# Turning, scaling and storing an expert's results later, and in three groups, in a mixture-of-experts kernel

## The chip, the cores and the metric

The kernel runs on one core of one Trainium2 chip. The metric is the device time of one execution in microseconds (us). The core's engines are called as in the profile: PE is TensorE (matmul), PEld its weight load, DVE is VectorE, ACT is ScalarE, POOL is GpSimd, and SP is the engine that issues most of the DMA transfers. SPq, ACTq and so on are the sequencers of these engines.

## The reference

There are 2048 tokens (8 batches of 256) of width 1024. Each batch is multiplied by one of eight adapter matrices; the result goes through a feed-forward block with one shared expert and 16 routed experts, two for each token, and is added to x.

```python
y = einsum('bsi,boi->bso', x, weight[itok])          # (8, 256, 1024), one adapter for each batch
gu_s = y2 @ shared_w_gate_up.T                       # y2: (2048, 1024)
shared = (silu(g_s) * u_s) @ shared_w_down.T         # inner width 1024
probs = softmax(y2 @ gate_w.T)                       # 16 experts
topk_vals, topk_idx = top_k(probs, 2)                # combine: the two values, normed to sum 1
gu = einsum('th,eih->eti', y2, w_gate_up)            # inner width 256
out_e = einsum('eti,ehi->eth', silu(g) * u, w_down)
return x + einsum('eth,te->th', out_e, combine) + shared
```

All of it is fp32. The kernel does not compute every expert for every token: it gathers the tokens of each expert, and computes those alone.

## The kernel before

Every fp32 operand of a matmul is made into two parts, `hi` and `lo`: `split` casts the source to `hi` on ACT (L88) and subtracts on DVE (L89) to get `lo`. A product is three matmuls, hi x hi, hi x lo and lo x hi (`mm3`, L139 to L141).

The work comes in stages: the adapter products, and the shared expert for the first half of the tokens, with the routing between (up to about 444 us of the profiled span); then the routed experts, to about 745 us; then the shared expert for the second half of the tokens, and the sum of all parts.

The experts are taken in the order of their load, so that each place n in this order has a fixed number of columns, `CAPS[n]`: 304 for n = 0 down to 264 for n = 10, and 256 for the last five. In each turn of the main loop over n (L1216):

- `expert_rows(n + 2)` gathers the tokens' rows on POOL (L839).
- `expert_up(n + 1)` loads four gate/up weights (`wgu`), each through `load_w`, and makes the gate and up products of expert n + 1.
- `expert_out(n)` loads two down weights (`wd`) through `load_w` and makes the down products of expert n. Where `CAPS[n]` is over 256 this is `expert_down_columns`.
- `expert_yt(n + 2)` turns the gathered rows (L226, into the tile `tt`) and splits them (L88, L89, tile `yte`).

`load_w` (L118) issues a weight's DMA on SP, in the order of the loads (tile `st`, four buffers), and splits it into the tile `hl` (five and two buffers). Then it takes the next entry of the list `between` and runs it, so that its instructions stand behind the subtraction of that load on DVE:

```python
        end = split(hl[:, 0, :], hl[:, 1, :], st)
        work = between.pop(0) if between else None
        if work:
            with tc.issue_after(end):
                work()
```

`issue_after(x)` makes the instructions of the block that run on the engine of x stand behind x. Otherwise the order on each engine is made by a planner with a timeline of its own (`schedule_with_timeline_sim`), which takes the earlier instruction of the program among those that it holds ready. Loads can run several ahead of the products that use them.

`expert_down_columns` has the results of expert n with the tokens along the free axis. Eight products (128 result columns each, 48 matmuls in all) go through the banks `acc` (seven of them); ACT copies each into `ot` (L920). Then DVE turns the 32 x 32 blocks from `ot` to `o` in two instructions (L922), ACT multiplies each 32 tokens by the routing weight in place (L928, nine or ten instructions), and SP stores `o` to the DRAM table `os_d` in four DMAs (L936), one for each quarter of the partitions. `ot` lies in the first and `o` in the second of the two `raw` tiles: there is one of each for all experts. The trace names both `raw`.

The turnings stand right behind the copies. The scalings come by `between`: its six entries meet the six loads that follow `expert_out(n)`, the four gate/up weights of expert n + 2 and the two down weights of expert n + 1. The last three of them carry three, three, and the remaining scalings; the stores stand behind the last.

For n = 13 and 14, `between` is filled with other work (`block`, L1209), which writes into the `raw` tiles again.

Of the kernel before, what the change touches and what calls it, by code (L numbers as in the profile page):

```python
# [17 lines left out]
P = 128  # L18
# [17 lines left out]
ROW0 = [sum(ROWS[:n]) for n in range(E + 1)]  # L36
# [5 lines left out]
def adapter_moe_kernel(ctx: ExitStack, tc: tile.TileContext, xT, x, itok, wc, gate, wgu, wd, sgu, sd, out):  # L42
    nc = tc.nc
# [27 lines left out]
    os_d = dram.tile([ZROW + 16, H], F32, tag="os_d", name="os_d")  # L71
# [7 lines left out]
    def bank():  # L79
        turn[0] += 1  # L80
        return banks[turn[0] % 7]
# [19 lines left out]
    between = []  # L101
# [36 lines left out]
    def mm3(ps, lhs, rhs, first, last):  # L138
        nc.tensor.matmul(ps, lhs[0], rhs[0], start=first, stop=False)  # L139
        nc.tensor.matmul(ps, lhs[0], rhs[1], start=False, stop=False)  # L140
        last_product[0] = nc.tensor.matmul(ps, lhs[1], rhs[0], start=False, stop=last).ins  # L141
# [705 lines left out]
    def expert_id(n):  # L847
        return nc.values_load(order[0:1, n : n + 1], engines=(mybir.EngineType.SP,), min_val=0, max_val=E - 1)
# [20 lines left out]
    def load_wd(e):  # L869
        return [load_w(wd[ds(e, 1), fi].rearrange("a p f -> p (a f)")) for fi in range(2)]  # L870
# [12 lines left out]
    def expert_down(po, at, w, off, c=1.0):  # L883
        o = po.tile([P, 1024], F32, tag="o", bufs=3, name="o")
        for h in range(2):
            ps = bank()
            for fi in range(2):
                mm3(
                    ps,
                    [at[:, l, fi, off : off + P] for l in range(2)],  # L890
                    [w[fi][:, l, h * 512 : (h + 1) * 512] for l in range(2)],
                    fi == 0,
                    fi == 1,
                )
            nc.scalar.activation(
                o[:, :].rearrange("p (a b j) -> p b a j", a=4, b=8)[:, 4 * h : 4 * h + 4],
                ps[:, :].rearrange("p (b a j) -> p b a j", b=4, a=4),
                AF.Copy,
                scale=c,
            )  # L900
        return o
# [3 lines left out]
    def expert_down_columns(n, at, w):  # L905
        m, rows, nt = CAPS[n], ROWS[n], ROWS[n] // 32
        ot, o = (r[:, :, :].rearrange("p c n -> p (c n)") for r in raw)
        ot = ot[:, : 8 * rows].rearrange("p (b t i) -> p b t i", b=8, i=32)
        o = o[:, : nt * 256].rearrange("p (t f) -> p t f", t=nt)
        for b in range(8):  # L910
            ps = bank()
            for fi in range(2):
                mm3(
                    ps[:, :m],
                    [w[fi][:, l, b * P : (b + 1) * P] for l in range(2)],
                    [at[:, l, fi, :] for l in range(2)],
                    fi == 0,
                    fi == 1,
                )
            nc.scalar.copy(ot[:, b], ps[:, :rows].rearrange("p (t i) -> p t i", i=32))  # L920
        for k in range(2):
            nc.vector.transpose(o[:, :, k * P : (k + 1) * P].rearrange("p t (b j) -> p b t j", b=4), ot[:, 4 * k : 4 * k + 4])  # L922

        def scaled(ts, end):
            def work():
                with tc.issue_after(last_cast[0]):
                    for t in range(nt)[ts]:
                        nc.scalar.activation(o[:, t], o[:, t], AF.Copy, scale=cwt[:, t, n : n + 1])  # L928
                if end:
                    store()  # L930

            return work

        def store():
            for a in range(4):
                nc.sync.dma_start(  # L936
                    os_d[ROW0[n] : ROW0[n] + rows, 256 * a : 256 * a + 256].rearrange("(t i) f -> i t f", i=32),
                    o[32 * a : 32 * a + 32],
                )

        between[:] = [None, None, None, scaled(slice(0, 3), False), scaled(slice(3, 6), False), scaled(slice(6, nt), True)]


    def segments(ix, ib):
# [45 lines left out]
    def expert_out(po, n, at):  # L990
        w = load_wd(expert_id(n))
        if CAPS[n] > MAIN:
            expert_down_columns(n, at, w)
            return
        for j in range(2):
            (nc.gpsimd if n > 13 else nc.sync).dma_start(os_d[ROW0[n] + j * P : ROW0[n] + (j + 1) * P, :], expert_down(po, at, w, j * P, cw[:, j, n : n + 1]))

# [13 lines left out]
    rows = {}  # L1011
# [7 lines left out]
    def turned(b, k):  # L1019
        return lambda: rows[b][k]()  # L1020
# [68 lines left out]
    t1 = up.operand_work("t1", 0, 1)  # L1089
# [76 lines left out]
    r0, rs = [], []  # L1166
# [49 lines left out]
    for n in range(E):  # L1216
        if n + 2 < E:
            rs = expert_rows(pa[1], n + 2)
        prev = at
        if n == 13:  # L1220
            with tc.issue_after(last_gather[0].ins):
                for k in range(2):
                    block_rows(k, spare())()
            between[:] = [None, None, block(0), None, block(1)]
        if n == 14:
            for k in range(4):
                block_rows(k + 2, spare() if k < 2 else tt[:, k % 2, :])()
            between[:] = [None, None, block(2), block(3), both(block(4), block_rows(6, tt[:, 0, :])), both(block(5), block_rows(7, tt[:, 1, :]))]
        if n + 1 < E:
            at = expert_up(pb[1], n + 1, nxt)  # L1230
        if n + 1 == E:
            close(pa)
            po = pool("po2", 4)
            ring = up.ring = po[1]
            op = up.begin_work()
            between[:] = [both(op[0], op[1]), op[2]]
        expert_out(pb[1], n, prev)
        if n + 2 < E:
            nxt = expert_yt((py if n % 2 else pa)[1], rs)
# [159 lines left out]
```

## Time and profile before

Three runs took 972.27, 974.15 and 976.29 us.

| | |
|---|---|
| median of the three runs | 974.15 us |
| the profiled execution | 981.36 us |
| its span in the profile | 979.2 us |
| mean granted TensorE clock | 0.994 |
| L920 copies | 88, median 0.413 us |
| L922 turnings | 22, median 1.372 us |
| L928 scalings | 101, median 0.496 us |
| L936 stores | 44: 36 of 288 KB, 8 of 320 KB |

The profile is of one execution, in microseconds from its span's start. A row of a timeline gives start, duration, engine, line, operation, written and read tiles and the number of instructions that were merged; what stands in brackets is the idle time of the engine before it, and what ended it. Instructions of ACT and DVE overlap a little, so nine scalings of 0.496 us in a row take 3.71 us. A DMA's row on SPq is the time that the issue takes; the data land later. Matmuls overlap too, so their pace is read from the distance of their starts: about 0.12 us for 264 columns.

### The profile page before, as it was taken

What the parts mean: (1) busy time and instruction counts of PE and PEld (TensorE: products, weight loads), DVE (VectorE), ACT (ScalarE), POOL (GpSimd) and SP (SyncE); (2) the same over time, 40 slices, a digit from 0 to 9 for tenths busy, and PEclk for the clock granted to TensorE, in tenths of its full rate; (3) what the DMA queues carried; (4) which work ended last, traced back from release to release, by engine and by line L of the source; (5) the groups of instructions that cost most, each with busy time, mean ns of one, the idle gap of its engine ahead of it and who ended that gap; (6) DMA issues with size and microseconds to landing.
All of it is one profiled execution on the core that took longest, in us unless ns stands there. A gap on an engine that the chain in (4) does not pass through costs nothing.

```text
span 979.2 us, 14565 instructions
## 1 busy us (share of the span) xinstructions
PE 962.2 (98%) x5183; PEld 834.5 (85%) x5183; DVE 715.3 (73%) x908; ACT 558.6 (57%) x819; POOL 309.2 (32%) x336
## 2 busy tenths in 40 slices
PE   8999999999999999999979999999999999999997
PEld 5888888888888888889969999999998888888886
DVE  4566888864779678649967888887878565969772
ACT  5556746566645452325758888878765465425440
POOL 2000200100074103666745556552001433330600
PEclk9999999999999999999979999999999999999999
DMA  8899967977799746868869989999997998994942
GB/s 299 283 322 356 372 209 278 370 252 246 247 213 259 164 126 134 295 233 260 243 221 286 309 279 287 299 308 321 310 328 263 326 355 310 272 263 127 250 147 100
DMA packets 92741, 257.62 MB, mean 263 GB/s; under 512 B 13298, under 2 KB 32514, under 8 KB 92658
## 3 DMA queue, kind: packets, MB, share of 16 engines
q1 hardware_dynamic: 60002, 173.04, 54.4%
q0 software_dynamic: 23056, 73.98, 23.9%
q10 hardware_dynamic: 9600, 9.57, 2.8%
q8 instruction: 42, 0.69, 0.3%
q14 instruction: 41, 0.34, 0.1%
HBM read 207.62 MB, written 48.93 MB: 262 GB/s over the span
## 4 chain that ended last, share of the span: by engine, by line
PE 94%; DMA 2%; issue 1%; DVE 1%; ACT 1%; SPq 0%; ACTq 0%
PE acc L530 31%; PE acc L141 19%; PE acc L139 19%; PE acc L140 19%; PE acc L731 5%; PE lp L286 1%; DMA st<-sd 1%; DMA st<-wc 1%; ACT hl L88 0%; DVE hl L89 0%; DVE shl L89 0%; ACT op L88 0%; DVE ca L759 0%; SPq L114 0%; DVE st L798 0%
## 5 line engine op out<-in xcount | busy, mean ns | idle before, releaser
L89 DVE TENSOR_TENSOR hl<-st,hl 128x1024 fp32r<-128x1024 f32 (+1 forms) x254 | 304.9, 1208 | 174.4 <-ACT hl L88 143.4
L88 ACT CAST hl<-st 128x1024 fp32r<-128x1024 f32 (+1 forms) x254 | 263.5, 1044 | 192.2 <-PE acc L141 70.6
L530 PE MATMUL acc<-op,hl 128*128 128x512 f32 x1296 | 298.0, 390 | 0.0
L530 PEld LDWEIGHTS acc<-op,hl 128*128 128x128 f32 x1296 | 242.4, 188 | 50.2
L839 POOL DMA_INDIRECT yg<-y_d,ix x128 | 155.2, 1213 | 80.1 <-issue 33.9
L141 PE MATMUL acc<-yte,hl 128*128 128x256 f32 (+6 forms) x512 | 147.2, 288 | 0.4 <-issue 0.4
L140 PE MATMUL acc<-yte,hl 128*128 128x256 f32 (+6 forms) x512 | 147.1, 287 | 0.3 <-issue 0.3
L139 PE MATMUL acc<-yte,hl 128*128 128x256 f32 (+6 forms) x512 | 147.3, 289 | 0.0
L140 PE MATMUL acc<-hl 128*128 128x512 f32 x256 | 100.3, 392 | 0.9 <-DVE hl L89 0.7
L141 PE MATMUL acc<-hl 128*128 128x512 f32 x256 | 99.7, 390 | 0.0
L141 PEld LDWEIGHTS acc<-yte,hl 128*128 128x128 f32 x512 | 96.3, 188 | 0.4 <-issue 0.4
L140 PEld LDWEIGHTS acc<-yte,hl 128*128 128x128 f32 x512 | 96.4, 188 | 0.2
L139 PEld LDWEIGHTS acc<-yte,hl 128*128 128x128 f32 x512 | 96.3, 188 | 0.2
L139 PE MATMUL acc<-hl 128*128 128x512 f32 x256 | 90.4, 391 | 1.5 <-ACT hl L88 1.5
L140 PEld LDWEIGHTS acc<-hl 128*128 128x128 f32 x256 | 48.0, 188 | 12.9 <-DVE hl L89 3.0
L139 PEld LDWEIGHTS acc<-hl 128*128 128x128 f32 x256 | 47.7, 188 | 12.3 <-ACT hl L88 2.5
L386 POOL DMA_INDIRECT tab_d<-tid,places x32 | 39.8, 1244 | 56.3 <-DVE ranks L372 46.8
L141 PEld LDWEIGHTS acc<-hl 128*128 128x128 f32 x256 | 48.1, 188 | 9.8
L139 PE MATMUL acc<-at,hl 128*128 128x264 f32 (+5 forms) x176 | 52.6, 299 | 2.7 <-issue 2.1
L141 PE MATMUL acc<-at,hl 128*128 128x264 f32 (+5 forms) x176 | 52.0, 295 | 2.5 <-issue 2.5
L140 PE MATMUL acc<-at,hl 128*128 128x264 f32 (+5 forms) x176 | 52.4, 298 | 1.3 <-issue 1.3
L141 PE MATMUL acc<-hl,ht 128*128 128x512 f32 x128 | 50.0, 391 | 0.0
(234 smaller groups left out, 1454.6 us busy)
## 6 DMA issues: line engine op xcount, KB each, us to landing
st<-wgu SPq DMA_DIRECT2D x64, 512.0 KB
st<-wc SPq DMA_DIRECT2D x63, 512.0 KB
st<-wd SPq DMA_DIRECT2D x32, 512.0 KB
st<-ss_d SPq DMA_DIRECT2D x30, 512.0 KB
st<-sd SPq DMA_DIRECT2D x30, 512.0 KB
st<-sgu SPq DMA_DIRECT2D x24, 512.0 KB
os_d<-raw SPq DMA_DIRECT2D x36, 288.0 KB
yr<-y_d POOLq DMA_DIRECT2D x20, 512.0 KB
```

What stands on the lines that cost most here:

```text
L88: last_cast[0] = nc.scalar.copy(hi, src).ins
L89: last_split[0] = nc.vector.tensor_tensor(lo, src, hi.bitcast(F32), op=ALU.subtract).ins
L139: nc.tensor.matmul(ps, lhs[0], rhs[0], start=first, stop=False)
L140: nc.tensor.matmul(ps, lhs[0], rhs[1], start=False, stop=False)
L141: last_product[0] = nc.tensor.matmul(ps, lhs[1], rhs[0], start=False, stop=last).ins
L286: nc.tensor.matmul(lp[:, n0 : n0 + n], gpk[:, c * 2 * E : c * 2 * E + P], get(c)[l], start=(c == 0 and l == 0), stop=(c == NC - 1 and l == 1),
L386: i = nc.gpsimd.indirect_dma_start(out=tab_d[:, :], out_offset=bass.IndirectOffsetOnAxis(ap=places[r][:, tb : tb + 1], axis=0), in_=tid[r] ...
L530: last_product[0] = nc.tensor.matmul(ps, lhs[x], rhs[y], start=(first and c == 0 and i == 0), stop=(c == 3 and i == 2), skip_group_check=T ...
L731: nc.tensor.matmul(ps[k], lhs[x], rhs[y], start=(first and t == c == i == 0), stop=(t == c == 1 and i == 2), skip_group_check=True,)
L839: last_gather[0] = nc.gpsimd.indirect_dma_start(out=r[:, t * 256 : (t + 1) * 256], out_offset=None, in_=y_d.rearrange("k a p f -> (k a p) f"),
```

## The change

Between two of these experts the order of three pieces of work changes.

- The two turnings of expert n are no longer right behind its copies. They become entries of `between` and meet the two down weights of expert n + 1.
- The scalings of expert n are kept back in `rest_of` when its down products are done, and come into `between` one expert later: they meet the first three gate/up weights of expert n + 3.
- Each of the three groups of scalings (three, three and the remaining) is followed by its own four stores, of its own rows. So there are twelve stores for an expert, and 132 for all eleven.

For the first expert the first three entries are empty. When the experts of 256 columns begin (n = 11), the last scalings that were kept back become the entries of the next loads.

```diff
-        for k in range(2):
-            nc.vector.transpose(o[:, :, k * P : (k + 1) * P].rearrange("p t (b j) -> p b t j", b=4), ot[:, 4 * k : 4 * k + 4])
-
-        def scaled(ts, end):
+        def turned(k):
+            return lambda: nc.vector.transpose(o[:, :, k * P : (k + 1) * P].rearrange("p t (b j) -> p b t j", b=4), ot[:, 4 * k : 4 * k + 4])
+
+        def scaled(t0, t1):
             def work():
                 with tc.issue_after(last_cast[0]):
-                    for t in range(nt)[ts]:
+                    for t in range(t0, t1):
                         nc.scalar.activation(o[:, t], o[:, t], AF.Copy, scale=cwt[:, t, n : n + 1])
-                if end:
-                    store()
+                r0, r1 = ROW0[n] + 32 * t0, ROW0[n] + 32 * t1
+                for a in range(4):
+                    nc.sync.dma_start(
+                        os_d[r0:r1, 256 * a : 256 * a + 256].rearrange("(t i) f -> i t f", i=32), o[32 * a : 32 * a + 32, t0:t1]
+                    )
             return work
-        def store():
-            for a in range(4):
-                nc.sync.dma_start(
-                    os_d[ROW0[n] : ROW0[n] + rows, 256 * a : 256 * a + 256].rearrange("(t i) f -> i t f", i=32),
-                    o[32 * a : 32 * a + 32],
-                )
-        between[:] = [None, None, None, scaled(slice(0, 3), False), scaled(slice(3, 6), False), scaled(slice(6, nt), True)]
+        between[:] = (rest_of[0] or [None] * 3) + [None, turned(0), turned(1)]
+        rest_of[0] = [scaled(0, 3), scaled(3, 6), scaled(6, nt)]
+
+    rest_of = [None]
...
         if CAPS[n] > MAIN:
             expert_down_columns(n, at, w)
             return
+        if rest_of[0]:
+            between[:], rest_of[0] = rest_of[0], None
         for j in range(2):
```

## The prediction

> **What bounds the kernel now.** I read the page first, then TensorE's pace in the expert stage, then the round that the change touches, engine by engine.
>
> ```profile
> span 979.2 us, 14565 instructions
> PE 962.2 (98%) x5183; PEld 834.5 (85%) x5183; DVE 715.3 (73%) x908; ACT 558.6 (57%) x819; POOL 309.2 (32%) x336
> ...
> PE 94%; DMA 2%; issue 1%; DVE 1%; ACT 1%; SPq 0%; ACTq 0%
> ```
>
> TensorE is busy all the time and is 94% of the chain that ended last. This edit leaves every matmul as it is, so it can only take away the stalls between them, or add some. The windows view says where stalls lie in the stage of the eleven big experts (475 to 690):
>
> ```profile
> 488.00:492.00 4.00, 2.82 (x17) 2.29 (x16) 0.74 (x1) 0.00 (x0) 3.09 (x4) 1.00 0.95 329
> 492.00:496.00 4.00, 1.30 (x3) 0.76 (x3) 0.00 (x0) 0.00 (x0) 2.96 (x4) 0.59 1.03 331
> 496.00:500.00 4.00, 1.95 (x6) 1.42 (x6) 1.67 (x3) 2.12 (x4) 0.95 (x1) 0.50 0.54 211
> 519.00:617.00 98.00, 98.00 (x774) 98.00 (x773) 85.37 (x97) 82.76 (x162) 54.85 (x46) 1.00 0.90 294
> 617.00:654.00 37.00, 35.69 (x290) 35.27 (x290) 30.86 (x34) 29.37 (x58) 19.83 (x16) 1.00 0.91 304
> 654.00:690.00 36.00, 36.00 (x282) 35.03 (x282) 30.72 (x33) 29.85 (x56) 11.43 (x10) 1.00 0.91 309
> ```
>
> The columns are stretch, length, then busy time and count of PE, PEld, DVE, ACT and POOL, granted clock, DMA share. From 519 on TensorE is full but for 617 to 654. In the timeline of TensorE two matmul starts there are 0.93 and 0.94 us apart instead of 0.12, at 633.4 (down columns of expert 8) and 651.9 (expert 9): 0.81 + 0.82 = 1.6 us. The waits put the second on the copies of L920. The other loss is 488 to 503: 26 matmuls in the first three rows, where 12 us at the usual 0.134 hold 90, so 64 x 0.134 = 8.6 us, and about 1.1 more until the clock is back. The profile names no cause for it ("issue").
>
> What made ACT late at 633 is a round through the tile `o`, here for expert 7 (DVE, then ACT, then SP's queue, from the timeline):
>
> ```profile
> 620.02 1.38 DVE L922 STREAM_TRANSPOSE raw<-raw 128x1152 f32<-128x1152 f32 x1 [2.79 <-DMA os_d<-raw]
> ...
> 623.55 1.37 DVE L922 STREAM_TRANSPOSE raw<-raw 128x1152 f32<-128x1152 f32 x1
> ...
> 624.95 3.71 ACT L928 ACTIVATE raw<-raw,cwt 128x256 f32<-128x256 f32 x9 [1.29 <-DVE raw L922]
> ...
> 631.98 2.00 ACT L88 CAST yte<-tt 128x1024 fp32r<-128x1024 f32 x2
> 633.88 0.39 ACT L920 COPY raw<-acc 128x288 f32<-128x288 f32 x1
> ...
> 628.69 4.02 SPq L936 DMA_DIRECT2D os_d<-raw  x4
> 632.95 0.80 SPq L123 DMA_DIRECT2D st<-wgu  x1
> ```
>
> The turning may not write `o` until expert 6's stores have landed: DVE stood 2.79 us. The nine scalings start when both turnings are done; the stores start when all nine are done (628.69) and are issued by 632.71; the next turning is at 637.51. So a round is turnings 4.9 (620.02 to 624.92, two other DVE instructions between) + scalings 3.7 + issue 4.0 + landing and start 4.8 = 17.4 us, and 17.5 by the starts. TensorE needs 144 matmuls x 0.122 = 17.6 us for an expert of 264 columns. L922 starts at 524.96 for expert 2 and at 675.02 for expert 10: 18.8 us a round. The waits view has 5.7 us in 4 places on DVE for these stores. Each pushes scalings, casts and in the end L920 back.
>
> **The change part by part.** The sums are made against the profiled execution (981.36 us: span 979.2 and 2.2 around it). It is 7.2 us above the median of 974.15; less the 9.7 us of 488 to 503 it is 971.7, so ordinary runs seem to have that stretch rarely or in part. What I find I take off the median.
>
> *Turnings moved.* Two L922 an expert, 1.38 us each, go from behind the columns to behind the splits of the next expert's two down weights. Those splits run ahead of TensorE: expert 9's end at 633.82 and 641.11, and expert 8's turnings run at 637.51 and 641.03 today. So the place in time hardly changes; what changes is that they yield to earlier program work. 0 us, bounded by one turning either way (1.4 an expert). A new wait comes with it: the copies L920 of expert n+1 overwrite `ot` and must follow the turnings of n; behind L920 on ACT stand the casts, and TensorE waits for its bank. Cover: with loads, casts, splits and matmul groups counted off in order along the timeline, those down weights are split 5.2 us (expert 8's second: 623.63, used at 628.78) to 13 us ahead of their matmul, against 1.4 of turning. Without cover 11 x 1.4 = 15 us.
>
> *Scalings moved.* The 101 L928 (9 x 0.41 = 3.7 us an expert) go behind the casts of loads 1, 2 and 3 of the expert after next. Today's block of nine at 644.11 already stands behind the third of these casts (643.15), so the place is again near; but the casts (1.05 each) may now come between groups: 3.7 to 5.8 us from first to last. Expert 10's scalings move to expert 13's loads, where ACT is busy 38.86 of 54.91 us (665.09 to 720): hidden, 3.7 if not. Expert 0's (10 x 0.41) leave its round. 0 us in sum.
>
> *Stores in thirds.* 44 SP issues become 132, over the same bytes and 1 KB packets. One issue takes 0.33 to 0.45 us for the first two of a burst, more after (1.22 and 1.69 here), when earlier ones still drain. Twelve cost 4.0 to 5.4 us against 4.0 now, so SP has 0 to 1.4 us more an expert; but only four stand behind the last scaling, 1.4 to 1.8 us. Queued behind them are gate/up loads: today a load follows 0.24 us after the burst, so it was held; with thirds, loads can pass between. The split operands lead TensorE by 9 to 14 us for gate/up weights, so a load up to 1.4 us later is hidden: 0; without the cover 11 x 1.4 = 15 us. POOL's queue is passed by nothing.
>
> Here a rule speaks against the change: the Trainium skill, "DMA: Bandwidth & Descriptors", section "Anatomy of one DMA", fits a DMA (GpSimd's path) by 2.0 us + bytes / 436e3 per us, and its section "Bandwidth" says to batch to 1 MiB. By that fit a 96 KB third costs 2.2 us, and twelve one after another 27 us (estimate): the round would be 9 us over the 17.6 and nine rounds would lose some 80 us. The row: four stores of 288 KB, 2.7 us each by the fit, are issued in 4.0 us and the next turning starts 8.8 us after the first issue, not 10.7 plus; they overlap. I take the row: thirds are in flight together.
>
> *The round after it.* 4.9 + (3.7 to 5.8) + (1.4 to 1.8) + at most 4.8 = 14.8 to 17.3 us, so 0.2 to 2.7 shorter than 17.5. Where it is shorter, DVE's waits at L922 go, ACT's scalings end sooner, and L920 is in time at 633 and 651. Gain: the 1.6 us of TensorE stalls. Next late is nothing until TensorE's own 17.6. On the profiled execution 981.36 - 1.6 = 979.8; on the median 974.15 - 1.6 = 972.5.
>
> **The rivals.** About 0.5%, 4.9 us, is what a measurement of this kernel can tell from no change.
>
> *Nothing moves (974.2).* The places in time are those of today, as shown, and the stalls are L920 behind two yte casts (631.98, 2.00 us), which the edit does not touch. For it: at 651.9 no store wait came before (expert 8's L922 had none). Against: thirds start earlier whatever else happens.
>
> *A later landing blocks DVE (982).* The scalings have lost their rank: gate/up casts, yte casts and copies now precede them. If the last group slips, its stores land late, and DVE stands at the next L922 with the split of the second down weights behind it. DVE idles 98 - 85.37 = 12.6 us over five rounds, 2.5 a round, so a landing up to 2.5 us later a round is paid from that; beyond it the lead of 5 to 9 us is eaten. At 4 us later, 1.5 net x 10 rounds = 15, less 7 of lead: 8 us, 982. For it: ACT is busy 82.76 of 98 us and each group needs a cast first. Against: the 14.8 to 17.3 above. A second rule would add to this: "TensorE: Matmul & The Clock Gate", Part 1, halves the clock after about 3.4 us of idle. The rows agree at 492 (0.59 after sparse matmuls), but single stalls of 0.9 us left 1.00; with waits spread over rounds I add nothing, by the rule 1.7 us or more for each stall that long.
>
> *The stretch at 488 goes (964.5).* It begins as expert 0's stores are issued (486.57 to 490.73). If ordinary runs have it too, thirds may dissolve it: 974.15 - 9.7. Against: ten other bursts have no such stretch.
>
> **How the numbers follow.** Main case 0.42, nothing moves 0.22, both within 4.9 us: same 0.64. Blocked DVE 0.25, slower; the stretch goes 0.11, faster. Likeliest 972.5. Main case alone: 970 to 975. The range goes down to 967, leaving half of the last case out, and up to 982, leaving half of the blocked case: 0.055 + 0.125 = 0.18 outside.
>
> **What would show it.** Right: DVE's wait for os_d at the turning under 1 us in all, stores at SP in groups of four with loads between, no TensorE gap over 0.3 us from 600 to 660, turnings within 2 us of today's place in a round. Wrong: L922 waits for stores of over 2.5 us a round, L920 waiting for L922, gate/up loads stuck behind stores so that casts wait for DMA beyond today's 13 us (505 to 690), or matmul gaps in the columns of experts 4 to 10. If the stretch of half clock is there in one profile and not in the other, spans cannot be compared without it.

## The result, and the profile after

The changed kernel is slower: 978.02 us against 973.55 (medians of 20 runs each), a ratio of 1.0043 with an interval of 1.0031 to 1.0055. The prediction was 972.5 us, a little faster. With this many runs 0.43% can be told from no change, finer than the half per cent that the prediction reckoned with. In some later comparisons the kernel before itself took 982 to 987 us; each ratio below is therefore against the kernel before in the same comparison.

The page of the changed kernel: span, busy times, chain by engine and by line.

```profile
span 975.7 us, 14711 instructions
PE 960.3 (98%) x5183; PEld 833.9 (85%) x5183; DVE 715.9 (73%) x908; ACT 559.6 (57%) x819; POOL 310.8 (32%) x336
...
PE 85%; DMA 7%; ACT 2%; DVE 2%; issue 1%; SPq 1%; POOL 0%; ACTq 0%; DVEq 0%
PE acc L530 31%; PE acc L140 15%; PE acc L141 15%; PE acc L139 15%; PE acc L731 8%; DMA st<-wd 3%; PE lp L286 1%; ACT hl L88 1%; DMA st<-wgu 1%; DVE hl L89 1%; DMA st<-wc 1%; ACT raw L929 1%; SPq L932 1%; DMA os_d<-raw 1%; DMA gst<-gate 1%
```

TensorE carries 85% of the chain, where it was 94%; the weight loads, the scalings (L929 now) and the stores (L932) have come into it. The windows view says where (stretch, length, busy time and count of PE, PEld, DVE, ACT, POOL, granted clock, DMA share, GB/s):

```profile
488.00:500.00 12.00, 12.00 (x91) 12.00 (x90) 10.59 (x14) 9.33 (x17) 9.82 (x8) 1.00 0.99 342
...
519.00:617.00 98.00, 95.98 (x759) 95.54 (x758) 83.44 (x93) 79.53 (x157) 52.89 (x46) 1.00 0.90 289
617.00:654.00 37.00, 33.47 (x259) 32.84 (x258) 30.29 (x33) 29.11 (x57) 18.01 (x18) 0.95 0.91 284
654.00:690.00 36.00, 36.00 (x283) 35.04 (x282) 27.52 (x30) 28.10 (x52) 8.56 (x8) 1.00 0.84 255
```

The stretch of half clock at 488 is absent, so the shorter span (975.7 for 979.2) says nothing of the change. Between 519 and 654 TensorE now idles 5.55 us, where it idled 1.31. Taken from the distances of its starts, the stalls over 0.25 us from 510 to 690 add up to 6.4 us against 1.6: 0.3 at 588.6, 2.1 at 606.7, 0.6 at 626.5, 0.3 at 643.3 and 3.1 at 645.1. The difference, 4.7, is near the 4.5 of the medians, but it is not the whole account. The clock of 0.95 in the third row is a stretch of half clock, from 649.9 to 653.3, just behind the worst stall:

```profile
650.00:653.00 3.00, 3.00 (x16) 3.00 (x15) 3.00 (x3) 2.32 (x4) 1.31 (x2) 0.50 0.95 313
```

The matmuls in it lose 1.5 us against their usual distance, on top of the stalls. Over all timed runs the mean granted clock is 0.9970 in the changed kernel (20 runs) and 0.9985 in the kernel before (50 runs, those beside e15); 0.15% of 975 us is again 1.5 us, so about a third of the loss may lie in the clock (an estimate from these figures).

The waits view, 505 to 690 (us in total, places, longest), tells what was waited for; first before, then after, each in the order of its answer:

```profile
ACT hl L88 <- DMA st<-wgu: 13.1, 11, 3.2
...
DVE raw L922 <- DMA os_d<-raw: 5.7, 4, 2.8
```

```profile
ACT hl L88 <- DMA st<-wd: 26.2, 11, 5.1
...
PEld acc L139 <- ACT raw L920: 6.3, 4, 3.2
...
ACT hl L88 <- DMA st<-wgu: 6.2, 10, 1.5
...
DVE raw L922 <- DMA os_d<-raw: 1.4, 1, 1.4
```

TensorE waits for the copies of L920, as before. VectorE's wait for stores is nearly gone (5.7 before). But ScalarE now stands 32.4 us at casts for weight loads, where it stood 13.1, and all of the growth is for down weights. (This sum alone does not measure the loss: e17 below has 28.9 us of such waits and loses nothing.) Here is the worst stall, in the timelines of ScalarE and then SyncE's queue:

```profile
620.29 1.31 ACT L929 ACTIVATE raw<-raw,cwt 128x256 f32<-128x256 f32 x3
...
634.02 1.05 ACT L88 CAST hl<-st 128x1024 fp32r<-128x1024 f32 x1 [5.09 <-DMA st<-wd]
...
639.69 3.70 ACT L929 ACTIVATE raw<-raw,cwt 128x256 f32<-128x256 f32 x9
...
647.97 2.17 ACT L920 COPY raw<-acc 128x288 f32<-128x288 f32 x7
```

```profile
618.04 0.33 SPq L123 DMA_DIRECT2D st<-wd  x1
618.48 7.31 SPq L932 DMA_DIRECT2D os_d<-raw  x12
626.04 0.36 SPq L123 DMA_DIRECT2D st<-wd  x1
626.65 10.05 SPq L123 DMA_DIRECT2D st<-wgu  x4
```

One down load leaves at 618.04; then all twelve stores pass, 7.31 us, and only then the second down load, at 626.04. Its cast waits 5.09 us and runs at 634.02. Everything behind it on ScalarE is late: the next scalings, and at 647.97 the copies, for which TensorE has stood 3.1 us since 645.1. In the profile before, both down loads stood ahead of the four stores, which began at 628.69:

```profile
626.05 1.61 SPq L123 DMA_DIRECT2D st<-wd  x2
```

### The profile page after: what moved, and what is told of

Read it like the earlier page. It is cut to its first block, busy times and chain, and to the rows that moved or that the text cites. A ratio compares the mean times of both kernels' runs of the same rounds, so it can differ in the third digit from the quotient of the medians.

```text
span 975.7 us, 14711 instructions
## 1 busy us (share of the span) xinstructions
PE 960.3 (98%) x5183; PEld 833.9 (85%) x5183; DVE 715.9 (73%) x908; ACT 559.6 (57%) x819; POOL 310.8 (32%) x336
## 4 chain that ended last, share of the span: by engine, by line
PE 85%; DMA 7%; ACT 2%; DVE 2%; issue 1%; SPq 1%; POOL 0%; ACTq 0%; DVEq 0%
PE acc L530 31%; PE acc L140 15%; PE acc L141 15%; PE acc L139 15%; PE acc L731 8%; DMA st<-wd 3%; PE lp L286 1%; ACT hl L88 1%; DMA st<-wgu 1%; DVE hl L89 1%; DMA st<-wc 1%; ACT raw L929 1%; SPq L932 1%; DMA os_d<-raw 1%; DMA gst<-gate 1%
## 5 line engine op out<-in xcount | busy, mean ns | idle before, releaser
L88 ACT CAST hl<-st 128x1024 fp32r<-128x1024 f32 (+1 forms) x254 | 263.2, 1043 | 199.7 <-PE acc L141 74.0
L140 PEld LDWEIGHTS acc<-hl 128*128 128x128 f32 x256 | 48.0, 188 | 13.1 <-DVE hl L89 3.2
L139 PE MATMUL acc<-at,hl 128*128 128x264 f32 (+5 forms) x176 | 51.8, 294 | 5.5 <-ACT raw L920 5.3
L140 PE MATMUL acc<-at,hl 128*128 128x264 f32 (+5 forms) x176 | 51.2, 291 | 0.0
L141 PE MATMUL acc<-at,hl 128*128 128x264 f32 (+5 forms) x176 | 51.2, 291 | 0.0
```

Source lines behind the costliest of these rows:

```text
L88: last_cast[0] = nc.scalar.copy(hi, src).ins
```

## Experiments

Two numbers are set beside each ratio in the table. The *round* is the time from one block of scalings to the next on ScalarE, by their starts, averaged over the six rounds from expert 2's block to expert 8's. The *stalls* are TensorE's over 0.25 us from 510 to 690. The half clock is not in them: after, e1, e2, e3, e14 and e15 each have one stretch of it in that window, 3.4 us long, which costs 1.5 to 1.8 us more, and the other rows have none.

| kernel | scalings | stores on SyncE | round | stalls | ratio |
|---|---|---|---|---|---|
| before, three profiles | in a block | 4, behind both down loads | 18.9, 18.7, 19.3 | 1.6, 0.6, 5.2 | 1 |
| e17 | in a block | 8, for experts 0 to 6 ahead of the second down load | 18.9 | 2.8 | 0.9993 [0.9979, 1.0007] |
| e11, same kernel | in a block | 8 | 18.6 | 3.9 | 1.0017 [0.9989, 1.0044] |
| e2 | in a block | 12 | 19.8 | 6.5 | 1.0031 [1.0020, 1.0043] |
| e1 | cast inside | 4 | 19.5 | 6.2 | 1.0029 [1.0016, 1.0042] |
| e16 | cast inside | 8, for experts 0 to 6 with the second down load between the fours | 19.6 | 6.1 | 1.0042 [1.0029, 1.0056] |
| e12, same kernel | cast inside | 8 | 19.4 | 6.4 | 1.0073 [1.0043, 1.0102] |
| after | cast inside | 12 | 19.6 | 6.4 | 1.0043 [1.0031, 1.0055] |
| e15, same kernel | cast inside | 12 | 19.4 | 5.2 | 1.0036 [1.0021, 1.0051] |
| e13 | cast ahead | 4 | 19.1 | 6.4 | 1.0049 [1.0020, 1.0077] |
| e3 | cast inside | 12, behind both down loads | 19.8 | 6.9 | 1.0077 [1.0058, 1.0096] |
| e5 | cast inside | 4, ahead of a down load | 19.9 | 12.3 | 1.0086 [1.0066, 1.0107] |
| e14 | in a block | 4, and 8 tiny transfers | 21.1 | 20.5 | 1.0205 [1.0178, 1.0233] |

"Cast inside" is what the change does to ScalarE's order: the third gate/up cast stands between the sixth and the seventh scaling, for experts 0 to 7. (From expert 8 on it stands ahead of all nine, in the kernel before too.) TensorE itself needs 18.3 us a round here (the down products of expert 2 start at 509.0 in e17 and those of expert 9 at 636.8: seven rounds). The letters of theories are those of each quoted expectation.

**The parts apart: e1, e2.** e1 is the change with its stores as four again:

```diff
+                if t1 < nt:
+                    return
                 for a in range(4):
                     nc.sync.dma_start(
-                        os_d[r0:r1, 256 * a : 256 * a + 256]..., o[32 * a : 32 * a + 32, t0:t1]
+                        os_d[ROW0[n] : ROW0[n] + rows, 256 * a : 256 * a + 256]..., o[32 * a : 32 * a + 32]
```

> The changed kernel with its turnings and scalings where it has them, but the stores of an expert again in four DMAs behind the last group. On SP's queue the four then stand behind both down loads, as before the change. Theory P (the loss is the second down load's place behind the stores on SP): ratio to before 0.997 to 1.001, the cast of the second down weights no longer waits for its load (0 of the 26 us in the changed kernel), no TensorE gap over 1 us between 580 and 660. Theory S (twelve DMAs that share eight completion semaphores with the loads): the same ratio, 0.997 to 1.001, since there are four. Theory M (the moved turnings and scalings, and their lower rank): as slow as the changed kernel, 1.004.

e2 is the kernel before with the twelve stores and nothing moved:

```diff
-                if end:
-                    store()
+                t0, t1 = ts.start, ts.stop
+                r0, r1 = ROW0[n] + 32 * t0, ROW0[n] + 32 * t1
+                for a in range(4):
+                    nc.sync.dma_start(
+                        os_d[r0:r1, ...], o[32 * a : 32 * a + 32, t0:t1]
```

> The kernel before with nothing moved, only each group of scalings followed by its own four stores (twelve for an expert). On SP's queue the twelve now stand ahead of the second down load for most experts, and ahead of both for some. P: 1.003 to 1.006, casts of down weights wait some 20 us in all for their loads. S: 1.003 to 1.006 too. M: 0.999 to 1.001.

Each part alone costs 0.3%, and together they cost 0.4%: no single theory of the three holds, and the parts do not add. e1 has the turnings moved as well; they were not tried alone, but in the traces no copy waits for one. In e1 no down load is late, yet ScalarE waits for gate/up weights. Two answers, ScalarE's timeline and SyncE's:

```profile
632.47 1.05 ACT L88 CAST hl<-st 128x1024 fp32r<-128x1024 f32 x1 [3.89 <-DMA st<-wgu]
...
637.26 1.05 ACT L88 CAST hl<-st 128x1024 fp32r<-128x1024 f32 x1 [2.25 <-DMA st<-wgu]
638.22 3.70 ACT L929 ACTIVATE raw<-raw,cwt 128x256 f32<-128x256 f32 x9
```

```profile
620.61 3.47 SPq L933 DMA_DIRECT2D os_d<-raw  x4
624.32 8.07 SPq L123 DMA_DIRECT2D st<-wgu  x4
```

The last scaling of the block before ended at 620.58. So the four stores left at 620.61, the gate/up loads behind them from 624.32 on, and the cast of the first of these ran 8.2 us after its issue. This is a closed round that the prediction had not drawn: end of the scalings, stores on SyncE, loads behind them, casts of these loads on ScalarE, next scalings. The round through `o` is longer here as well: VectorE waits 10.2 us for stores at its turnings (5.7 before, 1.4 after), so e1 does not part the two rounds.

**The place of the down loads: e3, e5.** Both force SyncE's order in the changed kernel: e3 keeps twelve stores but lets both down loads go first, e5 has four stores and puts them ahead of the second down load.

```diff
+        sts = [fetch_w(wd[ds(e, 1), fi]...) for fi in range(2)]
+        with tc.issue_after(last_load[0].ins):
+            for store in stores:
+                store()
+        stores[:] = []
+        return [load_w(None, st=st) for st in sts]
```

> The changed kernel with its twelve stores, but both down loads are issued ahead of them on SP. P: 0.997 to 1.001; the casts of the down weights no longer wait for their loads. S: 1.003 to 1.006, the stores and the loads behind them still wait in turn for the landing of the DMA eight issues earlier. M: 1.004.

```diff
+        ahead, last_store[0] = last_store[0], None
+        return [load_w(wd[ds(e, 1), fi]..., behind=ahead if fi else None) for fi in range(2)]
```

> The changed kernel with four stores for an expert, and these put ahead of the second down load on SP by an order edge, as the twelve are. P: slower than before, 1.002 to 1.005 (the stores hold SP for some 4 us in place of 7.6), the cast of the second down weights waits for its load. S: 0.999 to 1.001, four stores do not come round the eight semaphores. M: 1.004, the same as with four stores behind both loads.

e3 cures the down loads and is slower than the changed kernel: the waits move to the next loads in the queue ("ACT hl L88 <- DMA st<-wgu" 32.6 us where after has 6.2). In e5 four stores wait for the last scaling with a down load behind them, and ScalarE waits 34.6 us for down weights. Whichever load is behind the stores is late. Both runs are slower than any of the three theories forecast.

**The kernel before, twice more: e6, e10.** No edit.

> The kernel before, once more, for a second profile. Its first profile held a stretch at 488 to 503 in which TensorE ran 9.7 us behind its usual pace, and loads and casts may have caught up in it. If that flattered it, ScalarE's waits for DMA from 505 to 690 come out nearer 20 than 13.1 us and TensorE's stalls in the experts' columns at 3 us or more; if not, both stay within 2 us of 13.1 and 1.6, and what the other kernels show above that is theirs. Time 973 either way.

> The kernel before, for a third profile. Both earlier ones held a stretch (488 to 503, 495 to 508) in which the granted clock fell and TensorE lost 7 to 10 us, so that loads and casts caught up. In a profile without such a stretch, theory A (stores on SyncE hold weight loads, and this is what the change made worse) wants SyncE's waits at the stores to stay at 2 to 6 us from 505 to 690, with none for st<-wd, TensorE's stalls at 1.5 to 4 us where the changed kernel has 6.4, and a span of 969 to 972. If the stalls come out at 6 or more as in the changed kernel, the stretch alone made the difference between the first two profiles, and the 4.5 us lie elsewhere.

All three profiles of the kernel before hold a stretch of lowered clock between 488 and 508 (8 to 10 us lost), and so do e11 to e13, which ran beside e10; after, e1, e2, e3, e5 and e14 to e17 hold none. e12 and e16 are one kernel, and only e12 has it. So the stretch goes with the occasion, not with this edit. e17 has ScalarE's whole order from the kernel before and no stretch, so the stalls of before without it are best read from e17: 2.8 us, not 1.6. ScalarE's waits for weight loads are 21.6 us in e6 and 13.6 in e10. e6 took 988.28 us, where 973 was expected, and its 5.2 us are mostly two stalls without a cause in the profile. e10 was meant as a profile without the stretch; it has one, and settles nothing.

**Stores away from SyncE: e7, e8, e9.** The four stores of before issued by GpSimd, the twelve of after by GpSimd, the four of before by ScalarE:

```diff
-                nc.sync.dma_start(
+                nc.gpsimd.dma_start(
```

> The kernel before, its four stores of an expert issued by GpSimd instead of SyncE. Theory Q: what costs time is stores and weight loads in one queue that issues in order, so with the stores elsewhere ScalarE's waits for DMA from 505 to 690 fall from 13.1 to under 8 us, TensorE's stalls to under 1 us, and the time is 971 to 973. Rival T: what matters is when the sixteen DMA engines move the bytes and when the buffers come free; the queue that issues is indifferent, so 973 with the waits as before. Rival G: GpSimd [...] stands behind its gathers, the stores leave later, VectorE waits at its turning for more than the 5.7 us of before, and the time is 975 or more.

> The changed kernel, its twelve stores of an expert issued by GpSimd instead of SyncE. Theory Q: the 4.5 us that the change cost are SyncE's issues of stores ahead of weight loads, so this kernel stands within 1 us of the one before with GpSimd's four stores, at 971 to 973; ScalarE's waits for DMA fall from 32.4 to under 10 us. Rival T: twelve small transfers and the moved scalings cost as much from any queue: 977 to 978. Rival G: twelve descriptor builds in GpSimd's queue hold its gathers of the next experts' rows, and the time is 980 or more.

> The kernel before, its four stores of an expert issued by ScalarE, behind its own last scaling. Theory Q: SyncE's queue is free for loads, which gives at most the 13.1 us of ScalarE's waits; but each of the four issues takes ScalarE's own time, some 0.3 to 0.5 us as on SyncE, so 1.2 to 2 us an expert come back on the engine that makes the casts: 972 to 974, with no wait for st<-wd or st<-wgu above 4 us in sum. Rival T: 973 with ScalarE's waits for DMA as before. Rival G': an issue on ScalarE waits for completions of earlier DMAs and holds the casts behind it: 976 or more.

All are slower: 1.0109 [1.0073, 1.0145], 1.0522 [1.0466, 1.0577] and 1.0340 [1.0283, 1.0397]. The part of Q on waits held: ScalarE's for weight loads fell to 4.9, 3.7 and 0.4 us. Its forecast of the time did not. In e8 the copies of L920 wait 18.7 us for VectorE's turnings and TensorE up to 6.3 us for the copies; in e9, whose profiled execution took 1028.36 us against a median of 1017.64, ScalarE waits 32.0 us for turnings. The round is 25.6 us in e8 and 22.9 in e9. For e7 it is 19.1 with stalls of 7.5 us, and VectorE's wait for stores is 10.6 us where e6, beside it, has 12.7; that does not make 1.1%, and its cause stays open.

**Eight stores: e11, e12, e16, e17.** Tiles 0 to 5 behind the second group of scalings, the rest behind the third: in the kernel before (e11, e17) and in the changed one (e12, e16).

```diff
-                if end:
-                    store()
+                if ts.start == 0:
+                    return
+                t0, t1 = (6, nt) if end else (0, 6)
```

> The kernel before, each expert's four stores split in two parts: tiles 0 to 5 behind the second scaling group, the rest behind the third; eight stores instead of four or twelve, nothing else changed. Theory A: SyncE's order comes out with the second down load behind all eight, as with twelve, so most of the loss of the twelve stays: 975 to 977, SyncE's waits for DMA st<-wd 15 us or more. Rival S: what costs is the ninth and later DMA in a row that waits for the eighth before it; with eight stores that is one wait at most, and the time is 973 to 974.5. Rival C: cost follows the count, half of the loss of twelve stores: 974.5.

> The kernel before with eight stores in two parts, the second down load behind all eight, once more. Place theory: 1.003, as with twelve. Number theory: half of the twelve stores' 0.31%, 1.0015. Cast theory: 1.000, and then the 1.0031 of the twelve stores is left to explain.

> The changed kernel with stores in two parts: none behind the first group, tiles 0 to 5 behind the second, the rest behind the third. On SyncE the second down load then stands between the two sets of four stores, which is what the prediction expected of the thirds. Theory A: that load leaves some 3 us earlier than behind twelve stores, and SyncE's waits at stores are those of the kernel with four stores and the moved cast; 975.5 to 976.5, under the changed kernel by 1.5 to 2.5 us. Rival C (count): between four stores (975.9) and twelve (978), so 977. Rival M (the moved cast alone is what costs): 976 whatever the stores.

> The changed kernel, on the same chip as the three others of this call: 1.003 to 1.0055 of before, as in its own comparison, by every theory.

> The changed kernel with eight stores in two parts, the second down load between them on SyncE, once more beside the changed kernel. Place theory: under the changed kernel by 1.5 to 2.5 us. Number theory: under it by some 1.5 us, a third of its loss. Cast theory (the third cast ahead of the last scalings is what costs, and what SyncE does is hidden): equal to the changed kernel, 1.004.

e16 and e17 ran in one comparison and came out as the cast theory had them; the place and number theories fell. With the scalings in a block, eight stores cost nothing (0.9993) although the second down load stands behind them for seven of the eleven experts; here SyncE's timeline of e17, two bursts, its waits from 505 to 690, and its block with the third gate/up cast behind it:

```profile
598.17 5.53 SPq L934 DMA_DIRECT2D os_d<-raw  x8
603.95 0.36 SPq L123 DMA_DIRECT2D st<-wd  x1
...
615.83 1.60 SPq L123 DMA_DIRECT2D st<-wd  x2
617.54 5.87 SPq L934 DMA_DIRECT2D os_d<-raw  x8
```

```profile
ACT hl L88 <- DMA st<-wgu: 15.8, 13, 3.6
...
ACT hl L88 <- DMA st<-wd: 13.1, 7, 3.2
```

```profile
595.63 3.71 ACT L928 ACTIVATE raw<-raw,cwt 128x256 f32<-128x256 f32 x9
599.25 1.03 ACT L88 CAST hl<-st 128x1024 fp32r<-128x1024 f32 x1
```

ScalarE waits 28.9 us for weights there, nearly as long as in the changed kernel, at no cost. In the changed kernel the same eight stores bring nothing: e16, with the second down load let through between the two fours, is at 1.0042 beside e15's 1.0036. In one comparison, then, the moved cast is worth 0.49 of a per cent with eight stores, 1.0042 less 0.9993, and the place of the down load alone is not the cause. On ScalarE the order of e16 differs from e17's up to expert 8 in that cast alone; on SyncE it differs in the place of the second down load and, once, of a gate/up load. e1 shows the same with four stores: behind both down loads, as in the kernel before, and 1.0029. Twelve stores look like a second, separate cost, which shows only without the cast (e2's 1.0031 against e17's 0.9993, from two comparisons).

**The cast ahead of the whole block: e13.** As e1, with all scalings at the third load.

```diff
-        rest_of[0] = [scaled(0, 3), scaled(3, 6), scaled(6, nt)]
+        rest_of[0] = [None, None, scaled(0, nt)]
```

> The changed kernel with four stores, and all nine scalings of an expert at the third load, so that the third gate/up cast stands ahead of the whole block instead of ahead of its last three. It also lets the planner set one load of gate/up ahead of the stores' place on SyncE. Theory A: the end of the block, and with it the stores and VectorE's next turning, is as late as with the cast ahead of three (1.05 us and its wait), so 975 to 977. Rival K: what cost 0.29% in the kernel with four stores was the gap inside the block, the cast waiting for its load with o half scaled; ahead of the block it costs nothing: 973 to 974.

1.0049 is against rival K, but it does not settle it. In this comparison the kernel before took 981.9 us, and the two other kernels in it came out 0.24 and 0.31 of a per cent higher than when they ran again (e11 and e17, e12 and e16); less that, e13 is near 1.002 (an estimate). Its order differs in more than the cast, too: for ten of the eleven experts a gate/up load stands ahead of the stores, and VectorE stood 7.5 us before two turnings without a cause in the profile. Whether it is the gap inside the block that costs, or that the block ends a cast later, stays open.

**Eight transfers more, without bytes: e14.** In the kernel before:

```diff
+            with tc.issue_after(last.ins):
+                for k in range(8):
+                    nc.sync.dma_start(cpad1[:96, 8 * k : 8 * k + 8], gate[:96, 0, :8])
```

> The kernel before, with eight more transfers on SyncE behind each expert's four stores: 96 rows of 32 bytes each from the gate's weights into an unused tile, 3 KB, so that SyncE issues twelve in a row as in the changed kernel, but both down loads stand ahead of them and no byte worth counting is added. Number theory: eight issues at 0.3 to 0.5 us, and waits for completions, keep the next four gate/up loads 3 to 5 us longer on SyncE; ScalarE's waits for st<-wgu rise from 13 to 25 us or more and the time is 975.5 to 978 where before is 973. Place theory (only a down load behind the stores costs): 973 to 974, since gate/up loads have the slack of 9 to 12 us that they have before TensorE needs them.

20 us slower, far beyond the number theory's 2.5 to 5. In its timeline of SyncE and its waits:

```profile
597.43 5.97 SPq L942 DMA_DIRECT2D cpad<-gate  x8
603.65 3.63 SPq L123 DMA_DIRECT2D st<-wgu  x4
```

```profile
ACT hl L88 <- DMA st<-wgu: 47.1, 12, 7.0
```

Both down loads are ahead, the transfers are 3 KB each, and the gate/up loads are merely held some 6 us longer. The round grows by 2.2 us. So the round is closed through SyncE, and a gate/up load that leaves 6 us late is not hidden.

**ScalarE relieved: e18, e19.** The first three scalings of an expert on GpSimd, in the kernel before and in the changed one:

```diff
+                        if t < 3:
+                            nc.gpsimd.tensor_scalar(o[:, t], o[:, t], cwt[:, t, n : n + 1], None, op0=ALU.mult)
+                        else:
```

> The kernel before, with the first three of an expert's nine or ten scalings made by GpSimd instead of ScalarE. Lead theory: ScalarE's block falls from 3.7 to 2.5 us, its round from 18.9 to some 17.7 us, under TensorE's 18.3; its lead at the start of the down columns stays at 2.5 us or more, TensorE's stalls of 1.5 to 3 us go, and the time is 0.997 to 0.999 of before. Rival G: GpSimd's scalings are far longer than ScalarE's 0.41 us (no trace here has one; from 0.4 to 3 us each), stand behind gathers, and hold the stores and VectorE's next turning: 1.003 or more. Rival L (loads bound the round, not ScalarE's work): 1.000, the time freed turns into waits for st<-wgu.

> The changed kernel with the first of its three scaling groups made by GpSimd. Lead theory: the 1.2 us given back to ScalarE are more than the 1 us that the third cast took inside the block, so most of the loss goes: 1.000 to 1.002. Rival L: the loss stays at 1.0035 to 1.0045, with longer waits for st<-wd. Rival G: 1.006 or more, the first four stores waiting for GpSimd with SyncE's loads behind them.

1.0256 [1.0219, 1.0292] and 1.0198 [1.0167, 1.0229]: rival G. The groups of GpSimd, its share of SyncE's waits, and VectorE's wait in e18:

```profile
L929 POOL TENSOR_SCALAR raw<-raw,cwt 128x256 f32<-128x256 f32 x27 | 44.9, 1674 | 3.4 <-issue 3.3
```

```profile
SPq L939 <- POOL raw L929: 20.2, 9, 4.8
```

```profile
DVE raw L922 <- DMA os_d<-raw: 27.6, 9, 5.8
```

A scaling takes 1.67 us there against 0.50 on ScalarE; the three end late, SyncE stands at the stores with the loads behind them, and ScalarE waits 50.3 us for weights. It is the same round, lengthened at another link. Whether relief of ScalarE would help, these runs cannot say. No version beat the kernel before.

## Why the prediction was wrong

- *Turnings moved, 0 us:* right as far as the traces show. VectorE's order of turnings is that of before, but for one that changed places with its neighbour, and no copy waits for a turning in the waits view.
- *Scalings moved, 0 us in sum:* this step failed. It called the new place "again near", because the block of nine at 644.11 already stood behind the third gate/up cast. That is expert 8's block, the first for which this holds. For experts 0 to 7 the cast came after the block, as here for expert 7, with expert 8 below it:

```profile
624.95 3.71 ACT L928 ACTIVATE raw<-raw,cwt 128x256 f32<-128x256 f32 x9 [1.29 <-DVE raw L922]
628.57 1.04 ACT L88 CAST hl<-st 128x1024 fp32r<-128x1024 f32 x1
...
643.15 1.05 ACT L88 CAST hl<-st 128x1024 fp32r<-128x1024 f32 x1 [1.27 <-DMA st<-wgu]
644.11 3.71 ACT L928 ACTIVATE raw<-raw,cwt 128x256 f32<-128x256 f32 x9
```

  So the edit put a cast in front of the last scalings of eight experts. The length from first to last was foreseen (3.7 to 5.8 us; 4.66 in the trace, one cast more than 3.71), but put at nothing. It costs 0.29% with four stores (e1) and 0.49% with eight (e16 less e17). The timeline of the changed kernel:

```profile
598.38 2.51 ACT L929 ACTIVATE raw<-raw,cwt 128x256 f32<-128x256 f32 x6
600.80 1.03 ACT L88 CAST hl<-st 128x1024 fp32r<-128x1024 f32 x1
601.74 1.31 ACT L929 ACTIVATE raw<-raw,cwt 128x256 f32<-128x256 f32 x3
```

  The block ends a cast later, and the round goes from 18.9 to between 19.4 and 19.6 us. From the end of a block to the start of the next expert's down products on TensorE ScalarE has a lead: 3.7, 3.1, 1.2 and -0.7 us at the down products of experts 2, 4, 7 and 9 in e17, and 2.7, 1.1, -1.8 and -2.3 in e16. The round of before is already some 0.6 us longer than TensorE's 18.3 and eats the lead by expert 9. With the cast inside, the lead begins 1 us shorter and is gone at expert 5 in e16 and at expert 6 in after (in e15 it falls from 0.1 to -4.8 at expert 9, at once); from there, or from the next expert on, TensorE stalls at L920. That may also be why the two parts do not add: either would use up the same lead. This link is read from the traces and not shown by an experiment; the one that should have lengthened the lead (e18) failed for another reason.
- *Stores in thirds, 0 us:* the second step that failed. Twelve issues took 5.7 to 8.2 us, not 4.0 to 5.4; no load passed between them; from the end of the last scaling to the last store it was 4.5 us (603.05 to 607.52), not 1.4 to 1.8. And "a load up to 1.4 us later is hidden" took its cover from the wrong place: 9 to 14 us is the lead of a split weight over the matmul that uses it, but the first to need the load is ScalarE's cast, with the scalings and copies behind it in order, and there the lead was 3.7 us early in the stage and gone at expert 9 (e17). e14 shows what a late gate/up load costs, for loads held some 6 us; a delay of 1.4 us was not tried.
- *The round after it, a gain of 1.6 us:* the round through `o` did get shorter (VectorE's wait 5.7 to 1.4 us), but it was not what made L920 late. e17 has no wait at all for stores at L922 and still stalls 2.8 us, some 5 us into the down products as before. The sum of 17.5 us was of one quick round; by the starts of the blocks the six from expert 2 to 8 average 18.9, and TensorE needs 18.3, not the 17.6 of the experts of 264 columns. So the round was the longer of the two already.
- *The rule weighed* (27 us for twelve in a row, the prediction's estimate): the row was the better guide, with 5.7 to 8.2 us to issue twelve; but they were not issued freely, as said below.
- *The clock, put at nothing for single stalls:* too low by 1.5 us. The stall of 3.1 us at 645.1 was followed by 3.4 us of half clock, and so were stalls of 2.0 to 3.1 us in e1, e2, e3 and e15. Not every stall of that length is: one of 3.1 us in e5 and one of 2.2 us in e16 left the clock at 1.00.
- *Rivals:* "nothing moves" fell, and a blocked VectorE did not come. "Gate/up loads stuck behind stores so that casts wait for DMA beyond today's 13 us" stood under the signs of being wrong, and came, with 32.4 us, for down loads; it should have been a rival on the slower side, with ScalarE as the engine held, though e17 shows that such waits by themselves need not cost. The stretch at 488 follows the occasion. That 978.02 lies within the range of 967 to 982 is luck: the range reached up there for the blocked VectorE.

## What to carry to other kernels

When a store shares an in-order queue with loads, draw the round through that queue: what the store waits for, which load stands behind it, which engine takes that load first, and what else that engine must do before the store's data exist again. Count the cover of a late load at its first consumer and at everything in order behind that, not at the matmul that uses the data in the end. An instruction put in front of the last piece that a store waits for can lengthen every round: here a cast of 1.03 us added 0.5 to 0.7. And when the order of one engine is read from a timeline, look at more than one round: the one that was read here was the exception.

## What was not expected of the hardware

The twelve stores are not issued evenly. In the trace SyncE's transfers signal on eight semaphores in turn, and the program lets each wait on its semaphore, so a transfer is held until the one eight places earlier has landed: the eighth store stopped for 2.0 us for the down load issued just ahead of the burst. It was issued at 605.26, and that load landed at 605.25. SyncE's waits, 505 to 690, in the changed kernel:

```profile
SPq L932 <- DMA st<-wd: 7.8, 7, 2.0
SPq L932 <- ACT raw L929: 7.1, 6, 2.6
```

The first row is absent in the kernel before and in e17, and 0.6 to 1.3 us in e11, e12 and e16; with twelve stores in e2 it is 10.1. That it is this stop that makes twelve stores cost 0.31% where eight cost nothing fits, but was not tried by itself. And eight transfers of 3 KB in rows of 32 bytes took SyncE 5.97 us, more than four stores of 288 KB in the kernel before (2.9 to 4.2): few bytes do not make an issue short. Whether it is the number of transfers or their small rows was not parted.
